# Attention scores of the last image in the scans' PSUM while a scan waits, and gates multiplied into the scans' sums

## The chip, the cores and the metric

The kernel runs on one core of one Trainium2 chip. The metric is the device time of one execution in microseconds (us); a kernel's time is the median of several runs. TensorE is written PE, VectorE DVE, ScalarE ACT, GpSimd POOL, and SyncE SP; SP issues nearly all DMAs here. PSUM has eight banks of 512 f32 per partition; SBUF has 128 partitions.

## What is computed

A batch of 4 images, each 32 x 32 x 256 in f32, that is 1024 rows of 256 channels, goes through four layers. Images meet nowhere.

```python
x = L0(x)   # norm, 256->512, depthwise 3x3, gelu; scan with 64 states per channel; norm, 512->256, add
x = L1(x)   # 1x1 256->128, grouped 3x3, 1x1 128->256, add, relu
t = t + attention(ln(t), edges)          # 8 heads of 32; the mask allows the given edges only
t = t + moe8(ln(t))                      # 8 experts of hidden 256, two chosen, all computed
# L3, attention slot: a scan with 16 states per channel
x_main, x_gate = split(ln(t) @ W_in)     # 512 channels each
u  = silu(x_main @ W_conv)
dt = softplus(u @ W_dt);  B, C = split(u @ W_bc)
h[t] = exp(dt[t] * A) * h[t-1] + dt[t] * B[t] * u[t]      # per channel and state
y[t] = sum over states of h[t] * C[t]
t = t + (y * silu(x_gate)) @ W_out
t = t + moe8(ln(t))                      # 8 experts of hidden 512
```

## The kernel before

**Two programs in one.** `Hybrid.run` writes one instruction stream from two Python generators. `scans` emits the eight recurrences one after the other, in the order of `SCANS`: (0,0), (0,1), (3,0), (0,2), (3,1), (0,3), (3,2), (3,3), a pair being layer and image. `STAGES` is the side work: `front` (L0 up to its scan), `middle` (the end of L0, L1, attention, the first experts, and L3 up to its scan, which is `front3`), and `last` (`back3`, then the second experts `moe(3, b, tb)` and the store of the image). At each `yield` of `scans`, `run` advances the side work by up to two ticks, as long as the estimated clocks of all engines (class `Metered`) stay behind that of DVE. So the order on every engine is fixed when the program is written.

**A scan's unit.** A unit is 128 partitions of (channel, state): 2 channels in layer 0, 8 channels in layer 3. There are 256 units in a scan of layer 0 and 64 in a scan of layer 3. For unit k the generator emits:

- `load(k)`, line 416: `dA`, the channels' dt rows, each spread over its states by a DMA of its own from SP: 2 DMAs in layer 0, 8 in layer 3. Tile `dA` has 5 buffers, so the DMAs of unit k wait until the scan of unit k-5 has been done.
- `decay(k)`: ACT takes exp of `dA` in place.
- `first(k)`: PE spreads dt*u from tile `S` into `ps_rep`, a tile of two PSUM banks (tag "x", 2 buffers: four banks).
- DVE multiplies `ps_rep` by the rows of B in place, and then makes the scan `h<-dA,ps_rep`; POOL multiplies `h` by the rows of C.
- `pair(k)`, for every second unit: PE sums over the states into `ps_y`. After the 8 units of a block of 64 channels (layer 3; 64 units in layer 0), ACT copies `ps_y` to `yo`, and SP stores it in DRAM (`y<-yo`, line 470, two DMAs).

In step k the order is `load(k + 4)`, `first(k + 1)`, `decay(k + 2)`, DVE's product for k, a yield, the scan and POOL's product for k, and, where k is odd, `pair(k - 2)`. So POOL has the product of unit k ahead of whatever `pair(k - 2)` gives it, and SP has `load(k + 4)` ahead of the stores of `pair(k - 2)` and `load(k + 5)` behind them.

**A scan that waits.** `chunk` loads tile `S` for a block of units, from `parts` that `front3` or `front` has written. Where these do not exist yet, and 5 units (`LATEST`) are left before them, `need` runs the side work to that point with no unit of a scan in between. This happens to (3,3): it waits for `middle` of image 3. The wait stands at the start of step 59 of scan (3,2).

**Attention of one pair of heads** (`heads`): for each of 8 blocks of keys, `scores` makes two score tiles `ps_sc` (tag "s", one bank each, 2 buffers) by three matmuls for each head (keys x queries in f32; the row maxima, in bf16; the mask, in bf16), and ACT takes exp of each into `p`. Then `values` adds four f32 matmuls with 32 columns of weights each (values and ones, for two heads) into `ps_at`. `pipe` emits `values` of a block before `scores` of the next one:

```python
for s in reversed(range(len(steps))):
    if 0 <= tick - s < len(items):
        steps[s](items[tick - s])
```

Four pairs of heads times two halves of the queries are eight calls for an image, 64 blocks of keys in all.

**The gate.** `front3` stores silu(x_gate) in DRAM as `gate`. `back3` loads it again for each of the four groups of 128 channels (`gate_back`, 512 KB each, line 1699), loads the sums (`y_back`, line 768), and POOL multiplies the one into the other in two halves (`gated`) before PE's projection `ps_o`.

Of the kernel before, what the change touches and what calls it, by code (L numbers as in the profile page):

```python
# [7 lines left out]
F32 = mybir.dt.float32  # L8
BF16 = mybir.dt.bfloat16
I32 = mybir.dt.int32  # L10
AF = mybir.ActivationFunctionType
ALU = mybir.AluOpType
# [4 lines left out]
P = 128  # L17
NB = 4
L = 1024
TB = L // P  # L20
C = 256
DI = 512
DC = DI // P
# [18 lines left out]
AHEAD = 12  # L42
LATEST = 5
# [89 lines left out]
class Hybrid:  # L133
# [217 lines left out]
    def scans(self, mp, psum):  # L351
# [14 lines left out]
            ]  # L366
        chunks, rows, waiting = {}, {}, []
        state = {}
        y = None

        def chunk(k):

# [21 lines left out]
                )  # L394
            chunks[scan, d] = S

        def chunks_ahead(k):

            if k + AHEAD < len(units) and units[k + AHEAD][2:] == (0, 0, 0):
                waiting.append(k + AHEAD)  # L400
            while waiting:
                scan, d = units[waiting[0]][:2]
                if waiting[0] - k > LATEST and ("parts", *scan, d) not in self.ready:
                    break
                chunk(waiting.pop(0))

        def load(k):
            if k >= len(units):
# [23 lines left out]
        def first(k):  # L432
            if k >= len(units):
                return
            scan, d, c, i, j = units[k]
            spread = self.tables[scan[0]][1]
            G = P // self.states[scan[0]]
            ps = psum.tile([P, L], F32, tag="x", name="ps_rep", bufs=2)
            for g in range(2):
                cols = slice(g * 512, (g + 1) * 512)  # L440
                nc.tensor.matmul(
                    ps[:, cols], lhsT=spread[:, i, :], rhs=chunks[scan, d][:, 2 * c + j, cols],
                    start=True, stop=True,
                )
            state[k] = (state[k], ps)

        def pair(k):

            nonlocal y
            scan, d, c, i, j = units[k]  # L450
            n = self.states[scan[0]]
            per = 32 * n // P
            collect = self.tables[scan[0]][2]
            if i == 0:
                y = psum.tile([P, 512], F32, tag="y", name="ps_y", bufs=1)
            h = [state.pop(k - 1), state.pop(k)]
            for g in range(2):
                for j in range(2):
                    at = 32 * (2 * g + j)
                    nc.tensor.matmul(  # L460
                        y[at : at + 32, :], lhsT=collect[:, i, :],
                        rhs=h[j][:, g * 512 : (g + 1) * 512],
                        start=(i == 0), stop=(i == per - 1), tile_position=(0, at),
                    )
            if i == per - 1:
                yo = mp.tile([P, 512], F32, tag="yo", name="yo", bufs=2)
                nc.scalar.copy(yo, y)
                to = self.keep(("y", *scan, d, c), [64, L])
                for g in range(2):
                    nc.sync.dma_start(to[:, g * 512 : (g + 1) * 512], yo[64 * g : 64 * g + 64, :])  # L470
                if c == 1:
                    self.done.add((scan, d))
# [6 lines left out]
        decay(1)  # L479
        first(0)  # L480
        for k in range(len(units) + 4):
            chunks_ahead(k)
            load(k + 4)
            first(k + 1)
            decay(k + 2)
            if k < len(units):
                a, inp = state.pop(k)
                B, Cm = rows[units[k][0]]
                nc.vector.tensor_tensor(inp, inp, B, ALU.mult)
            yield  # L490
            if k < len(units):
                h = mp.tile([P, L], F32, tag="h", name="h", bufs=5)
                nc.vector.tensor_tensor_scan(h, a, inp, 0.0, ALU.mult, ALU.add)
                nc.gpsimd.tensor_tensor(h, h, Cm, ALU.mult)
                state[k] = h
            if k % 2 == 1 and 2 <= k < len(units) + 2:
                pair(k - 2)
            yield

    def need(self, scan, d):  # L500
# [34 lines left out]
    def run(self):  # L535

        self.done, self.ready = set(), set()
        self.todo, self.stage, self.wait = list(STAGES), None, None
        nc, tc = self.nc, self.tc
        with tc.tile_pool(name="scan", bufs=1) as mp, tc.tile_pool(  # L540
            name="scps", bufs=1, space=PSUM
        ) as psum, tc.tile_pool(name="sdps", bufs=1, space=PSUM) as side, tc.manual_schedule():
            self.side_psum(side)
            self.mask_work, self.sorted = self.mask_prepare(), False
            clock = self.clock = dict.fromkeys(Metered.COST, 0.0)
            self.nc = Metered(nc, clock)
            for n, _ in enumerate(self.scans(mp, psum)):
                if n % 2:
                    next(self.mask_work, None)
                now = clock["vector"]  # L550
                for e in clock:
                    clock[e] = max(clock[e], now - LAG)
                for _ in range(TICKS):
                    if max(clock.values()) > clock["vector"] + LEAD or self.advance() is None:
                        break
            while self.advance() is not None:
                pass
            self.nc = nc
        assert not self.todo
# [742 lines left out]
    def heads(self, fp, raw, sums, qT, kT, v, maskT, mT, nh, hp):  # L1302

        nc = self.nc
        qs = slice(nh * 512, (nh + 1) * 512)
        c, at = hp // 2, 64 * (hp % 2)
        acc = self.psum.tile([P, 512], F32, tag="acc", name="ps_at", bufs=1)
        got = {}  # L1310

        def scores(kb):
            two = [self.psum.tile([P, 512], F32, tag="s", name="ps_sc", bufs=2) for _ in range(2)]
            rows = [slice(at + 32 * i, at + 32 * i + 32) for i in range(2)]
            for i in range(2):
                nc.tensor.matmul(
                    two[i], lhsT=kT[rows[i], c, kb * P : (kb + 1) * P], rhs=qT[rows[i], c, qs],
                    start=True, stop=False,
                )
            for i in range(2):  # L1320
                nc.tensor.matmul(
                    two[i], lhsT=self.onesb[rows[i], :], rhs=mT[rows[i], c, qs],
                    start=False, stop=False,
                )
            for i in range(2):
                nc.tensor.matmul(
                    two[i], lhsT=self.identb, rhs=maskT[:, kb, qs], start=False, stop=True
                )
            got[kb] = p = fp.tile([P, 2, 512], F32, tag="p", name="p", bufs=3)
            for i in range(2):  # L1330
                nc.scalar.activation(p[:, i, :], two[i], AF.Exp)

        def values(kb):
            p = got.pop(kb)
            for i in range(4):
                h = 2 * hp + i % 2
                nc.tensor.matmul(
                    acc[32 * i : 32 * i + 32, :],
                    lhsT=v[:, kb, h * HD : (h + 1) * HD] if i < 2 else self.ones,
                    rhs=p[:, i % 2, :],  # L1340
                    start=(kb == 0), stop=(kb == TB - 1), tile_position=(0, 32 * i),
                )

        yield from self.pipe(range(TB), scores, values, cost=1.3, cut=True)
        nc.scalar.copy(raw[at : at + 64, c, :], acc[:64, :])
        nc.scalar.copy(sums[at : at + 64, c, :], acc[64:, :])

# [343 lines left out]
    def back3(self, b, tb):  # L1691
        nc, tc = self.nc, self.tc
        with tc.tile_pool(name=f"h{b}", bufs=1, side="right") as sp:
            nc.sync.dma_start(tb, self.mem["t", b])
            y = sp.tile([P, DC, L], F32, name="y_back")
            gate = sp.tile([P, DC, L], F32, name="gate_back")

            def fetch(d):
                nc.sync.dma_start(gate[:, d, :], self.mem["gate", b, d])
                yield from self.scanned((3, b), y, d)  # L1700

            def gated(d):
                for g in range(2):
                    cols = slice(g * 512, (g + 1) * 512)
                    nc.gpsimd.tensor_tensor(y[:, d, cols], y[:, d, cols], gate[:, d, cols], ALU.mult)
                    yield 0.8

            yield 1.0
            yield from fetch(0)
            w_out = self.weight(sp, "L3_attn_W_out", DC)  # L1710
            yield from self.add_rows(tb, self.bout3, TB)
            for d in range(1, DC):
                yield from fetch(d)
                for _ in range(4):
                    yield 0.5
                yield from gated(d - 1)
            for _ in range(4):
                yield 0.5
            yield from gated(DC - 1)
            got = {}  # L1720

            def project(j):
# [95 lines left out]
```

## Time and profile before

| | |
|---|---|
| median of 3 runs | 6822.12 us (6815.66 to 6823.56) |
| profiled execution | 6818.64 us, of which the span of its instructions is 6816.9 us |
| busy, share of the span | PE 79%, DVE 77%, POOL 54%, ACT 51% |
| TensorE clock granted, mean | 0.828 |
| exp of scores, `p<-ps_sc` 128x512 | 512 times, 594 ns |
| POOL, `y_back<-y_back,gate_back` 128x512 | 32 times, 1266 ns (median) |
| POOL, `h<-h,rows` 128x1024 | 1280 times, 2372 ns |
| DMA issues of `dA` | 2048 of 256 KB and 2048 of 64 KB |
| attention of image 3, `ps_sc` | from 5505.4 to 5764.0 us |

Nearly every instruction has line 124, a wrapper through which all engines are called. So groups are told apart by their tiles' names, and only DMA issues by their lines. In a row of the timeline the first two numbers are the start and the length in us, and "[2.80 <-PE ps_sc L124]" means that the engine had been idle for 2.80 us and that PE's work on `ps_sc` ended this. An f32 matmul is recorded as two instructions, a bf16 matmul as one.

### The profile page before, as it was taken

The page shows a single profiled execution, that of the slowest core. Times are in us where ns is not written, and L with a number is a line of the kernel's source. Part 1 is how long each engine was busy: PE and PEld are TensorE (multiplying, and loading weights), DVE is VectorE, ACT ScalarE, POOL GpSimd, SP SyncE. Part 2 cuts the span into 40 slices and gives each one's busy share as a digit, 9 for nine tenths or more (in the row PEclk, how much of TensorE's full clock was granted, in tenths as well). Part 3 has the DMA queues.
Part 4 walks back from the last instruction along what each step waited for, and adds up shares of the span by engine and source line. Part 5 has one row for each costly group of instructions (what it writes and reads, how often), then busy time and mean ns, then how long its engine had stood idle before and what let it go on. Part 6 is the DMA issues. An engine that isn't in the chain of part 4 may idle for free. (4 is left out here: it accounts for less than half of the span.)

```text
span 6816.9 us, 65916 instructions
## 1 busy us (share of the span) xinstructions
PE 5387.2 (79%) x20320; PEld 2164.2 (32%) x20320; DVE 5225.0 (77%) x4486; ACT 3449.8 (51%) x4152; POOL 3651.6 (54%) x1801
## 2 busy tenths in 40 slices
PE   6558778579797568979689679798698687967979
PEld 3003213122242022234145222243253222523556
DVE  8778988988798987889889977798899861247411
ACT  2426666445476334557568345477485443245411
POOL 0876786755457655555856555557666540054200
PEclk8558779689798578979789689798698789877989
DMA  2556665754365665446756655366666640146321
GB/s 72 147 144 161 178 173 154 194 138 119 102 169 162 182 156 143 115 120 177 192 144 163 178 150 129 103 161 169 171 170 178 155 117 7 45 134 148 84 62 34
DMA packets 394235, 937.44 MB, mean 138 GB/s; under 512 B 83220, under 2 KB 165728, under 8 KB 392224
## 3 DMA queue, kind: packets, MB, share of 16 engines
q1 hardware_dynamic: 391696, 930.53, 51.3%
q8 instruction: 172, 2.82, 0.2%
q0 software_dynamic: 2128, 2.13, 0.2%
q14 instruction: 239, 1.96, 0.1%
HBM read 842.59 MB, written 93.95 MB: 137 GB/s over the span
## 5 line engine op out<-in xcount | busy, mean ns | idle before, releaser
L124 POOL TENSOR_TENSOR h<-h,rows 128x1024 f32<-128x1024 f32 x1280 | 3032.7, 2372 | 1995.8 <-DVE h L124 1649.5
L124 DVE TENSOR_TENSOR_SCAN h<-dA,ps_rep 128x1024 f32<-128x1024 f32 x1280 | 2925.3, 2285 | 238.9 <-issue 105.6
L124 DVE TENSOR_TENSOR ps_rep<-ps_rep,rows 128x1024 f32<-128x1024 f32 x1280 | 1552.9, 1213 | 289.0 <-PE ps_rep L124 288.8
L124 ACT ACTIVATE dA<-dA,A_L_conv_A_log 128x1024 f32<-128x1024 f32 x1024 | 1153.5, 1145 | 727.9 <-DMA dA<-dt 673.5
L124 PE MATMUL ps_rep<-S,spread_L_conv_A_log 96*128 96x512 bf16 x2048 | 765.6, 465 | 743.6 <-DVE h L124 710.4
L124 PE MATMUL ps_y<-h,collect_L_conv_A_log 128*32 128x512 f32 x4096 | 802.2, 761 | 95.5 <-POOL h L124 93.5
L124 PE MATMUL ps_h<-xTm,we 128*128 128x512 f32 x1536 | 719.0, 607 | 3.8 <-ACT h_m L124 2.2
L124 PE MATMUL ps_e<-we,h_m 128*128 128x256 f32 x3072 | 702.3, 381 | 8.1 <-ACT h_m L124 6.4
L124 ACT ACT_TABLE_LOAD x495 | 635.1, 1283 | 74.8 <-PE ps_h L124 44.3
L124 PEld LDWEIGHTS <-spread_L_conv_A_log 96*128 96x128 bf16 x2048 | 161.5, 103 | 1523.6 <-DVE h L124 1220.7
L124 PEld LDWEIGHTS ps_e<-we,h_m 128*128 128x128 f32 x3072 | 581.3, 190 | 155.4 <-issue 45.7
L124 ACT ACTIVATE p<-ps_sc 128x512 f32<-128x512 f32 x512 | 277.8, 594 | 549.9 <-PE ps_sc L124 537.4
L124 DVE SCALAR_TENSOR_TENSOR tb<-ps_e,cw,tb 128x256 f32<-128x256 f32 x512 | 220.6, 474 | 404.3 <-PE ps_e L124 404.3
L124 ACT ACTIVATE h_m<-ps_h,cols 128x512 f32<-128x512 f32 x384 | 260.7, 687 | 473.6 <-PE ps_h L124 470.9
L124 ACT ACTIVATE dA<-dA,A_L_attn_A_log 128x1024 f32<-128x1024 f32 x256 | 293.3, 1148 | 384.8 <-DMA dA<-dt 342.8
L124 PE MATMUL ps_at<-p,v 128*32 128x512 f32 x1024 | 374.6, 610 | 64.6 <-ACT p L124 53.8
L124 PEld LDWEIGHTS ps_h<-xTm,we 128*128 128x128 f32 x1536 | 291.7, 193 | 341.4 <-issue 294.2
L124 PE MATMUL ps_rep<-S,spread_L_attn_A_log 96*128 96x512 bf16 x512 | 184.4, 449 | 195.2 <-DVE h L124 177.1
L124 PE MATMUL ps_sc<-qT,kT 32*128 32x512 f32 x1024 | 295.2, 649 | 44.8 <-ACTq L1234 26.0
L124 PE MATMUL ps_at<-p,ones 128*32 128x512 f32 x1024 | 272.1, 610 | 0.0
L124 PEld LDWEIGHTS ps_y<-h,collect_L_conv_A_log 128*32 128x32 f32 x4096 | 107.4, 119 | 492.4 <-POOL h L124 243.3
L124 PE MATMUL ps_cv<-pad,diag 128*128 128x512 f32 x576 | 260.4, 593 | 0.0
(306 smaller groups left out, 4945.8 us busy)
## 6 DMA issues: line engine op xcount, KB each, us to landing
dA<-dt SPq DMA_DIRECT2D x2048, 256.0 KB
dA<-dt SPq DMA_DIRECT2D x2048, 64.0 KB
we<-in_L_ffn_W_dram SPq DMA_DIRECT2D x64, 512.0 KB
parts<-parts SPq DMA_DIRECT2D x64, 384.0 KB
S<-parts SPq DMA_DIRECT2D x96, 256.0 KB
dt<-sp_r SPq DMA_DIRECT2D x64, 256.0 KB
y<-yo SPq DMA_DIRECT2D x128, 128.0 KB
y_back<-y SPq DMA_DIRECT2D x64, 256.0 KB
```

The source lines that it names most:

```text
L124: return got(*args, **kw)
```

## The change

1. **Scores in the scans' PSUM.** `chunks_ahead` no longer stops at the start of step k. Where the `parts` are missing it says so, the step goes on without `first(k + 1)`, and at the end of the step the wait is made, with `self.alone` set, and then `first(k + 1)`. A call of `heads` that begins meanwhile puts the scores of both heads into one tile of tag "x" (`ps_sx`, two banks, two buffers), takes exp of both in one activation of 128x1024, and emits through a pipe with an empty step, so that `values` of a block comes behind `scores` of the next one.
2. **Gates beside the scan.** In `pair`, a scan of layer 3 loads a tile `gate` (128x512, one buffer; two DMAs of 128 KB) at the first pair of each block of 64 channels, and POOL multiplies it into `yo` behind ACT's copy; the stores follow. `back3` neither loads nor multiplies gates any more; `W_out` is loaded first there, and the ticks of the multiplications are gone.

The order of the instructions shows which work is affected: 40 of the kernel's 256 blocks of keys go over (80 of 512 score tiles, 40 activations `p<-ps_sx`), that is the last five of image 3's eight calls; 32 POOL products `y_back` become 32 products `yo`; 16 loads `gate_back` become 64 loads `gate_y`. The number of matmuls stays the same. The last unit of (3,2) whose input `ps_rep` is emitted before the wait is number 59 in both programs (units counted from 0), and the side work has 8027 matmuls ahead of that point before and 8007 after, 10 of them to a block of keys.

```diff
@@ scans
+        self.scan_psum = psum
+        y = gate = None
...
-        def chunks_ahead(k):
-            if k + AHEAD < len(units) and units[k + AHEAD][2:] == (0, 0, 0):
+        def chunks_ahead(k, late=False):
+            if not late and k + AHEAD < len(units) and units[k + AHEAD][2:] == (0, 0, 0):
                 waiting.append(k + AHEAD)
             while waiting:
                 scan, d = units[waiting[0]][:2]
-                if waiting[0] - k > LATEST and ("parts", *scan, d) not in self.ready:
-                    break
+                if ("parts", *scan, d) not in self.ready:
+                    if waiting[0] - k > LATEST:
+                        break
+                    if not late:
+                        return True
+                    self.alone = True
                 chunk(waiting.pop(0))
+                self.alone = False
+            return False
...
             if i == 0:
                 y = psum.tile([P, 512], F32, tag="y", name="ps_y", bufs=1)
+                if scan[0] == 3:
+                    gate = mp.tile([P, 512], F32, tag="gate", name="gate_y", bufs=1)
+                    for g in range(2):
+                        nc.sync.dma_start(
+                            gate[64 * g : 64 * g + 64, :],
+                            self.mem["gate", scan[1], d][64 * c : 64 * c + 64, g * 512 : (g + 1) * 512],
+                        )
...
                 nc.scalar.copy(yo, y)
+                if scan[0] == 3:
+                    nc.gpsimd.tensor_tensor(yo, yo, gate, ALU.mult)
...
-            chunks_ahead(k)
+            waits = chunks_ahead(k)
             load(k + 4)
-            first(k + 1)
+            if not waits:
+                first(k + 1)
...
                 pair(k - 2)
+            if waits:
+                chunks_ahead(k, True)
+                first(k + 1)
             yield
@@ heads
+        alone = self.alone
...
-            two = [self.psum.tile([P, 512], F32, tag="s", name="ps_sc", bufs=2) for _ in range(2)]
+            if alone:
+                both = self.scan_psum.tile([P, 2, 512], F32, tag="x", name="ps_sx", bufs=2)
+                two = [both[:, i, :] for i in range(2)]
+            else:
+                two = [self.psum.tile([P, 512], F32, tag="s", name="ps_sc", bufs=2) for _ in range(2)]
...
+            if alone:
+                nc.scalar.activation(p, both, AF.Exp)
+                return
             for i in range(2):
                 nc.scalar.activation(p[:, i, :], two[i], AF.Exp)
...
-        yield from self.pipe(range(TB), scores, values, cost=1.3, cut=True)
+        if alone:
+            yield from self.pipe(range(TB), scores, lambda kb: None, values, cost=1.3)
+        else:
+            yield from self.pipe(range(TB), scores, values, cost=1.3, cut=True)
@@ back3
             y = sp.tile([P, DC, L], F32, name="y_back")
-            gate = sp.tile([P, DC, L], F32, name="gate_back")
-
-            def fetch(d):
-                nc.sync.dma_start(gate[:, d, :], self.mem["gate", b, d])
-                yield from self.scanned((3, b), y, d)
-
-            def gated(d):
-                for g in range(2):
-                    cols = slice(g * 512, (g + 1) * 512)
-                    nc.gpsimd.tensor_tensor(y[:, d, cols], y[:, d, cols], gate[:, d, cols], ALU.mult)
-                    yield 0.8
-
-            yield 1.0
-            yield from fetch(0)
             w_out = self.weight(sp, "L3_attn_W_out", DC)
+            yield 1.0
+            yield from self.scanned((3, b), y, 0)
             yield from self.add_rows(tb, self.bout3, TB)
             for d in range(1, DC):
-                yield from fetch(d)
-                for _ in range(4):
-                    yield 0.5
-                yield from gated(d - 1)
+                yield from self.scanned((3, b), y, d)
             for _ in range(4):
                 yield 0.5
-            yield from gated(DC - 1)
```

More of the change, by code (lines that the diff above doesn't have):

```diff
@@ L368, in scans @@
         state = {}
-        y = None
+        self.scan_psum = psum
+        y = gate = None
         def chunk(k):
@@ L447, in pair @@
         def pair(k):
-            nonlocal y
+            nonlocal y, gate
             scan, d, c, i, j = units[k]
@@ L538, in run @@
         self.todo, self.stage, self.wait = list(STAGES), None, None
+        self.alone = False
         nc, tc = self.nc, self.tc
@@ L1324, in scores @@
                 )
+            got[kb] = p = fp.tile([P, 2, 512], F32, tag="p", name="p", bufs=3)
             for i in range(2):
@@ L1328, in scores @@
                 )
-            got[kb] = p = fp.tile([P, 2, 512], F32, tag="p", name="p", bufs=3)
+            if alone:
+                nc.scalar.activation(p, both, AF.Exp)
+                return
             for i in range(2):
@@ L1695, in back3 @@
             y = sp.tile([P, DC, L], F32, name="y_back")
-            gate = sp.tile([P, DC, L], F32, name="gate_back")
-            def fetch(d):
-                nc.sync.dma_start(gate[:, d, :], self.mem["gate", b, d])
-                yield from self.scanned((3, b), y, d)
-            def gated(d):
-                for g in range(2):
-                    cols = slice(g * 512, (g + 1) * 512)
-                    nc.gpsimd.tensor_tensor(y[:, d, cols], y[:, d, cols], gate[:, d, cols], ALU.mult)
-                    yield 0.8
+            w_out = self.weight(sp, "L3_attn_W_out", DC)
             yield 1.0
-            yield from fetch(0)
-            w_out = self.weight(sp, "L3_attn_W_out", DC)
+            yield from self.scanned((3, b), y, 0)
             yield from self.add_rows(tb, self.bout3, TB)
             for d in range(1, DC):
-                yield from fetch(d)
-                for _ in range(4):
-                    yield 0.5
-                yield from gated(d - 1)
+                yield from self.scanned((3, b), y, d)
             for _ in range(4):
                 yield 0.5
-            yield from gated(DC - 1)
             got = {}
```

## The prediction

> **What bounds the kernel now.** I read the 40 slices first, then the chain that ended last, then the timeline and the waits of the stretches that the change touches. In the slices, DVE is busy for some 80% up to slice 32; then the scans have nothing to do:
>
> ```profile
> PE   6558778579797568979689679798698687967979
> ...
> DVE  8778988988798987889889977798899861247411
> ```
>
> DVE's scans follow each other with gaps of at most 18 us, save one: unit 58 of (3,2) starts at 5592.1, unit 59 at 6048.8. In between, image 3 runs alone; its last five calls of `heads` fill the time from 5607.1 (ACT's copy `raw`) to 5766.5, the copy of the last call: 159.3 us. The table of busy time by stretch (us, then PE, PEld, DVE, ACT, POOL, clock, DMA share, GB/s):
>
> ```profile
> 5600.00:5767.00 167.00, 144.58 (x688) 36.45 (x684) 11.07 (x18) 55.57 (x102) 7.55 (x6) 1.00 0.01 2
> 6071.00:6385.00 314.00, 231.61 (x844) 105.45 (x845) 245.40 (x202) 157.60 (x163) 171.89 (x82) 0.76 0.61 157
> ```
>
> PE looks full in the first row, but the timeline of one block of keys shows a loop through ACT:
>
> ```profile
> 5626.46 1.13 PE L124 MATMUL ps_sc<-qT,kT 32*128 32x512 f32 x4
> 5627.42 0.38 PE L124 MATMUL ps_sc<-mT,onesb 32*128 32x512 bf16 x2
> 5627.74 0.60 PE L124 MATMUL ps_sc<-maskT,identb 128*128 128x512 bf16 x2
> 5628.22 1.09 ACT L124 ACTIVATE p<-ps_sc 128x512 f32<-128x512 f32 x2 [2.80 <-PE ps_sc L124]
> 5628.87 1.10 PE L124 MATMUL ps_at<-p,v 128*32 128x512 f32 x3 [0.53 <-ACT p L124]
> ...
> 5630.35 1.13 PE L124 MATMUL ps_sc<-qT,kT 32*128 32x512 f32 x4
> ```
>
> Scores, exp, values, scores: 3.89 us a block, all on the path, since nothing else can go on.
>
> Afterwards the chain is PE's experts to the end, with one hole where image 3's last stage begins:
>
> ```profile
> 6510.21 4.44 DMA out_dram<-tb
> ...
> 6517.48 10.01 DMA gate_back<-gate
> 6527.50 10.22 DMA y_back<-y
> 6537.88 1.27 POOL y_back L124
> ```
>
> In the scans of layer 3, SP is nearly full: eight issues a unit. In (3,1), 3873 to 4179 us, it waited for a free `dA` only this long (us, times, longest), and elsewhere issues stand end to end:
>
> ```profile
> SPq L416 <- DVE h L124: 17.5, 17, 3.6
> ```
> ```profile
> 4111.15 1.09 SPq L470 DMA_DIRECT2D y<-yo  x2
> 4112.34 8.44 SPq L416 DMA_DIRECT2D dA<-dt  x16
> ```
>
> **The change part by part**, against the profiled execution (6818.64 us; its span is 6816.9, the median of the runs 3.5 above it).
>
> *Scores.* With values a block later, PE has in order: scores k, values k-1, scores k+1, values k. Scores issue from 5626.46 to the second mask matmul's end of issue, 1.71 us (three matmuls of two heads; the next weights could go at 5628.17). Values that had `p` in time, earlier in the same attention, took 0.97, from 5523.40 to 5524.37:
>
> ```profile
> 5523.40 0.60 PE L124 MATMUL ps_at<-p,v 128*32 128x512 f32 x2
> 5523.41 0.60 PE L124 MATMUL ps_at<-p,ones 128*32 128x512 f32 x2
> ```
>
> So PE's floor is 2.69 us a block. The one exp of 128x1024 has no row from PSUM; the two halves took 1.09 together, `dA` of the same width 1.15. I take 1.15, at no cost: it lies beside values and scores of 2.69 us. Where that cover is gone, at the end of each call, PE waits about 0.45. Five calls: 40 x 2.69 + 5 x 0.45, plus 3.7 for `ps_wo` between them, are 113.6 instead of 159.3: **-45.7**. Bounds: nothing gained, if ACT still ends each block; -50.
>
> The row that bears on the clock is the first of the table: granted 1.00 throughout, although PE pauses 0.53 us in each block. A rule speaks against this part. The Trainium skill's page "TensorE: Matmul & The Clock Gate", section "A second HAM failure mode: psum-queue depth-cycling", says that going round PSUM banks can leave PE such short pauses that its clock swings between half and full; at half clock the 40 blocks would take 215 us, and the sum would turn to a loss. I go by the row.
>
> *Side work two blocks behind.* Ahead of the same unit 59 there are 8007 matmuls of side work instead of 8027, two blocks of keys. They now run in the wait, two by 3.89, less what the scans save without them (3.6 instead of 4.3 us for two units): **+6.4**, bounds 0 and 7.8.
>
> *Unit 59 before the wait.* One unit less after it, 6048.80 to 6052.23: **-3.4**; at worst 0.
>
> *Gate, into the scans.* Per block of 8 units SP gets two issues more (1.1, as the stores' 1.09) and its stores wait longer: for POOL's product (1.27 and 0.15 of signalling) behind ACT's copy, or behind POOL's `h` of unit k where that is later. Behind the waiting stores are `load(k + 5)` and all later ones; ACT's `decay` and then the scan wait for these. From the trace's times of the copies and of `h`, the stores of the four scans are released 11.5, 11.5, 11.8 and 8.1 us later in sum; with 8.8 for the issues each scan has about 20 us more on SP. Not all of it is lost: SP pays back where it waited for a buffer, and `dA` lies ready 2 to 5 us before its scan in quiet units, 7 to 18 behind side work on DVE. Carried from unit to unit by these two numbers, the lag delays the scans by 7, 7, 4 and 8 us: **+26**. Bounds 0 and 78. The gate's own DMAs wait for the product of the block before (one buffer), which the stores ahead of them have waited for already. On POOL, the product holds up `h` of unit k+1: by 1.3 us, and where ACT's copy comes late (it ended up to 5.2 us after `h` of unit k) by up to 2.8. I cost this at nothing, since POOL was busy for 170 us of 306 in (3,1), PE takes that `h` only three steps later, and `h` has five buffers; without that room PE, which reads `ps_y`'s inputs in order, would lose 1 to 3 us a block, which I leave within the upper bound.
>
> *Gate, out of `back3` of image 2.* Between 6109 and 6165 the scan (3,3) waits for `dA` behind `tb`, `W_out`, `y_back` and `gate_back`:
>
> ```profile
> 6152.53 2.29 DVE L124 TENSOR_TENSOR_SCAN h<-dA,ps_rep 128x1024 f32<-128x1024 f32 x1 [5.16 <-DMA dA<-dt]
> ```
>
> DVE's gaps there sum to 25 us. Gates are 2 of 5.5 MB; but the three last `y_back` pairs now come in one clump. I take a third, **-8**, bounds 0 and -25. The stage's ticks fall from 33 to 13, yet the order puts only 8 more matmuls before the scan's last unit; 24 are 13.8 us in the experts' stretch behind it: at most -4.6, I take **-3**. In images 0 and 1 the ticks come out even again within the scan, and DVE had its `dA` there: 0, within 5 either way.
>
> *Image 3's `back3`.* 5.5 MB landed from 6514.7 to 6537.7, 0.24 MB/us; 3.5 MB take 14.6 us, and the product of 1.27 goes too. PE starts `ps_o` at about 6529.5 instead of 6539.2: **-9.7**, bounds -1.4 and -12. Late next is PE itself.
>
> Sum: -45.7 + 6.4 - 3.4 + 26 - 8 - 3 - 9.7 = -37.4; 6781 for a profiled execution, 6785 for the median.
>
> **Rivals.** (a) *SP bounds the scans of layer 3.* If what SP gets more is lost whole, 78 instead of 26, the sum is +14.6: 6837, slower. For it: 17.5 us of waiting in 306, less than the 20 that come. Against: `dA` was mostly ready ahead of its scan, and DVE's stalls for side work give SP time. It decides from 16 us a scan on. (b) *Scores gain half*: the exp ends PE's waits after all, or weight loads keep a block at 3.3 us; then -23 there and -15 in all, 6807, at the edge of what a measurement tells. For it: PE's floor is put together from two places; against: both were recorded in the same attention at full clock. (c) *The gate is free*: 5-deep `dA` swallows everything, and the clump costs nothing: -63 to -75, about 6753. (d) That the change doesn't do what it says is excluded: the order has the forty activations of 1024.
>
> **How the numbers follow.** Forecast 0.66, (a) 0.11, (b) 0.11, (c) 0.12. The forecast's own range, with 38 to 50 for the scores and 12 to 40 for the gate, is 6767 to 6807. The range reaches up towards (a) and down over (c): 6750 to 6820 leaves out (a) and a few of the rest. About 0.2%, 13.6 us, is what a measurement tells from no change. Faster: forecast, (c) and a share of (b), 0.80; same: the rest of (b) and the low part of (a), 0.10; slower 0.10.
>
> **What would show it.** After: a block in the wait from one `ps_sx` score to the next in 2.7 us, ACT's exp about 1.1 long without PE idle before `ps_at`; the wait's gap in DVE some 40 us shorter than 456.7; scans (3,0) and (3,1) at 318 and 313 us up to the start of the next scan, instead of 310.6 and 305.9; SP's waits for `DVE h` there gone, and waits of line 470 for POOL; PE's `ps_o` of image 3 about 20 us after the store of image 2. Wrong: half clock in the wait, blocks above 3.3 us, or scans of layer 3 longer by 16 us or more.

## The result, and the profile after

The changed kernel takes 6839.83 us (median of 9 runs, 6828.76 to 6856.88), the kernel before 6822.12 beside it: a ratio of 1.0031, 95% interval 1.0019 to 1.0043. It is slower by 0.3%. The profiled execution has a span of 6834.1 us against 6816.9, that is 17.2 more, at a granted clock of 0.826 against 0.828.

The slices look as before; the scans' long hole on DVE is in the 34th and 35th:

```profile
PE   6558778679797567979789668798698678867989
...
DVE  8778988988798986789899977788899871247511
```

Stretch by stretch, from the starts of DVE's scans (the first two columns give the time from a scan's first unit to the next scan's first):

| stretch | before | after | difference |
|---|---|---|---|
| start to the first scan | 207.4 | 204.9 | -2.5 |
| (3,0) | 310.6 | 326.2 | +15.6 |
| (3,1) | 305.9 | 326.7 | +20.8 |
| (0,0), (0,1), (0,2), (0,3) together | 4491.9 | 4491.5 | -0.4 |
| (3,2), with the wait | 755.5 | 738.2 | -17.3 |
| (3,3), first to last unit | 306.1 | 323.3 | +17.2 |
| last unit of (3,3) to the end | 439.4 | 423.2 | -16.2 |

The wait does what it was to do. DVE's gap in it is 425.0 us instead of 456.7. The last five calls of image 3 take 125.8 us instead of 159.3 (ACT's copies `raw`, 5662.4 to 5788.2), and the timeline of PE has a block of keys from one score to the next in 2.81 us, with `values` of the block before behind the scores:

```profile
5715.98 1.13 PE L124 MATMUL ps_sx<-qT,kT 32*128 32x512 f32 x4
5716.95 0.38 PE L124 MATMUL ps_sx<-mT,onesb 32*128 32x512 bf16 x2
5717.26 0.60 PE L124 MATMUL ps_sx<-maskT,identb 128*128 128x512 bf16 x2
5717.80 0.62 PE L124 MATMUL ps_at<-p,v 128*32 128x512 f32 x2
...
5718.79 1.13 PE L124 MATMUL ps_sx<-qT,kT 32*128 32x512 f32 x4
```

Within a call PE no longer stops for `p`. The end does what it was to do as well. In the chain of the work that ended last there is no `gate_back` between the store of image 2 and `ps_o`, and from the one to the other it is 20.7 us instead of 29.0:

```profile
6534.98 4.47 DMA out_dram<-tb
6540.03 6.48 DMA w_L_attn_W_out<-in_L_attn_W_out_dram
6546.52 9.03 DMA y_back<-y
6555.69 14.34 PE ps_o L124 x58
```

All this is given away by the four scans of layer 3. What SP waited for in (3,1), at the stores before (3873 to 4179 us; total, times, longest):

```profile
SPq L470 <- ACT yo L124: 6.3, 4, 2.0
```

and at the stores and the loads after, 3885 to 4212 us:

```profile
SPq L489 <- POOL yo L124: 14.9, 5, 5.3
SPq L425 <- DVE h L124: 14.3, 8, 3.6
```

Line 489 is the stores of `yo`, 425 the loads of `dA`. The stores now wait for POOL's product, 15.3 us with all their waits instead of 6.5, and the 16 issues of `gate_y` take 9.5 us, counted from each start to the next: 18 us more on SP, and the scan is 20.8 longer. SP's wait for a free `dA` (`DVE h`) fell only from 17.5 to 14.3: some 3 us were paid back there. Where the engines lose the rest, by the waits of ACT and DVE in (3,1), before:

```profile
ACT dA L124 <- DMA dA<-dt: 73.0, 24, 8.3
...
DVE ps_rep L124 <- PE ps_rep L124: 30.4, 23, 6.7
DVE h L124 <- DMA dA<-dt: 13.2, 28, 7.8
...
DVE lnt_w L124 <- ACT lnt_r L124: 2.1, 1, 2.1
```

and after:

```profile
ACT dA L124 <- DMA dA<-dt: 95.3, 27, 7.7
...
DVE ps_rep L124 <- PE ps_rep L124: 38.4, 23, 12.2
DVE h L124 <- DMA dA<-dt: 13.3, 23, 4.9
DVE lnt_w L124 <- ACT lnt_r L124: 6.6, 1, 6.6
```

DVE itself waits no longer for `dA`. ACT does, 22.3 us longer, in the decays that stand two units ahead of the scan. DVE then waits for others: 8.0 us longer for PE's `ps_rep`, and 11 us longer ahead of its own side work (19.3 instead of 8.0 us over all such rows, of which the largest, `lnt_w`, is shown), where ACT or PE is late.

### The profile page after: what moved, and what is told of

It is laid out like the page before. It is cut to its first block, busy times and chain, and to the rows that moved or that the text cites. A ratio compares the mean times of both kernels' runs of the same rounds, so it can differ in the third digit from the quotient of the medians.

```text
span 6834.1 us, 65860 instructions
## 1 busy us (share of the span) xinstructions
PE 5346.9 (78%) x20236; PEld 2150.1 (31%) x20320; DVE 5219.0 (76%) x4486; ACT 3442.2 (50%) x4108; POOL 3649.1 (53%) x1801
## 5 line engine op out<-in xcount | busy, mean ns | idle before, releaser
L124 ACT ACTIVATE p<-ps_sc 128x512 f32<-128x512 f32 x432 | 234.4, 594 | 460.6 <-PE ps_sc L124 313.8
L124 PE MATMUL ps_at<-p,v 128*32 128x512 f32 x1024 | 352.7, 623 | 67.0 <-ACT p L124 59.3
L124 PE MATMUL ps_sc<-qT,kT 32*128 32x512 f32 x864 | 252.0, 657 | 50.4 <-ACTq L1258 43.6
```

Source lines behind the costliest of these rows:

```text
L124: return got(*args, **kw)
```

## The experiments

**Theory.** In the scans of layer 3 SP's new issues and its stores' wait are lost whole; scores and `back3` gain as meant. **Rivals**: the order of the side work has moved; POOL's product holds up the sums and the scans, whatever SP does; SP does pay back and something else costs.

Differences below are between the medians of a kernel and of the kernel before that was run beside it (6818 to 6821 us); in brackets stands the 95% interval of the ratio. The changed kernel's difference is +17.7. Lengths of scans are in us, measured as in the table above, from one profiled execution of each kernel. (0,3), which no edit of the kernel before, the changed one and the four parts touches, took 1134.2 to 1137.2 in these six, so differences of 3 us between scans say little.

### The change in parts

*Scores alone*: the diff's `chunks_ahead`, `heads` and the order in `scans`, with `back3` and `pair` as before.

> The kernel before with the scores' part of the change alone (back3 keeps its gates). Theory: the score part does what it was to do, only less, and costs the scans nothing: DVE's gap in the wait 32 to 40 us shorter than 456.7, the scans of layer 3 as long as before (310.6, 305.9), the median 28 to 38 us lower. Rival (the moved order of the side work, not the gates, makes the scans of layer 3 longer): (3,0) and (3,1) 10 us longer or more here too, and the median within 15 us of the kernel before.

6781.91 us, -37.5; ratio 0.9950 (0.9936 to 0.9963). Scans (3,0) and (3,1) take 310.2 and 309.3 us, DVE's gap in the wait 411.9 (behind unit 59 here, behind 58 before). The five calls take 121.2 us. The gap is 44.8 shorter, somewhat more than the theory said, and in (3,0) and (3,1) the order of the side work is not the cause. In (3,3) it may have a part: that scan takes 312.3 us instead of 306.1 without any gate in it.

*Gate alone*: `pair` and `back3` of the change, the rest as before.

> The kernel before with the gate part alone. Theory (SP is the bound in the scans of layer 3, so its new issues and waits are lost whole): each scan of layer 3 15 to 21 us longer, 65 to 70 in all, 16 less at the end; the median 42 to 55 us higher. Rival (as forecast, SP pays back): scans longer by 26 in all, median 5 us higher or less.

6876.80 us, +57.4; ratio 1.0085 (1.0072 to 1.0098). The scans are 19.2, 25.5, 20.4 and 13.0 us longer, 78 in sum, more than the 65 to 70 of the theory; the end is 20.5 shorter. Scores and gate alone sum to +19.9, the change to +17.7: the two parts hardly meet.

*Loads alone*, and *product alone*, each in the kernel before:

```diff
@@ loads alone: pair
+                if scan[0] == 3:
+                    gate = mp.tile([P, 512], F32, tag="gate", name="gate_y", bufs=1)
+                    for g in range(2):
+                        nc.sync.dma_start(gate[64 * g : 64 * g + 64, :], ...)
@@ product alone: scans, pair
+        one = mp.tile([P, 512], F32, name="one_y")
+        nc.gpsimd.memset(one, 1.0)
...
                 nc.scalar.copy(yo, y)
+                if scan[0] == 3:
+                    nc.gpsimd.tensor_tensor(yo, yo, one, ALU.mult)
```

> The kernel before with the loads of gate_y in pair alone: 64 DMAs more, nothing reads them, back3 keeps its gates. Theory: SP's issues are the bound, 16 x 0.58 = 9.3 us for each scan of layer 3, 30 to 40 us in all, at the median too. Rival 1 (POOL's product and the waits for it make all of the loss): 0 to 8 us. Rival 2 (SP pays back half from its waits for a free buffer): 15 to 22 us.

> The kernel before, with POOL multiplying yo by a tile of ones in the scans of both layers ahead of the stores; no gate is loaded, back3 keeps its gates. Theory: the stores wait 8 to 15 us longer in each scan of layer 3, in front of the loads of dA, and this is lost too: 25 to 40 us in all; together with the loads alone about the loss of the gate part's scans, 65 to 70. Rival (only issues count, the wait falls where SP would have waited for a free buffer): 0 to 8 us.

(The second text says "both layers"; the edit has the product in layer 3 alone.) Loads: 6858.95 us, +39.6; ratio 1.0063 (1.0050 to 1.0076); the first three scans longer by 5.2, 10.1 and 10.1 us, (3,3) by 10.1. Product: 6865.02, +45.7; ratio 1.0078 (1.0065 to 1.0091); scans longer by 12.5, 13.8, 8.5 and -0.9, and SP's wait at the stores in (3,1) is 17.5 us instead of 6.5. Behind the last unit of (3,3) the product's kernel loses another 12.0 us, to which no run here gives a cause. So 16 issues a scan, 9.5 us of SP, cost about that much (35.5 in the four scans), and one product of 1.27 us per block about as much (33.9). Both rivals that named a single culprit fail.

### Taking the load off SP again

*Stores later* (in the changed kernel): `pair` puts its stores on a list, and they are issued two units later.

```diff
-                for g in range(2):
-                    nc.sync.dma_start(to[:, g * 512 : (g + 1) * 512], yo[64 * g : 64 * g + 64, :])
+                def out(to=to, yo=yo, scan=scan, d=d, c=c):
+                    ...
+                late.append((k + 4 if scan[0] == 3 else k + 2, out))
@@ scans, behind pair(k - 2)
+            while late and late[0][0] <= k:
+                late.pop(0)[1]()
```

> The changed kernel with the stores of yo in layer 3 put two units later on SP, behind two more loads of dA, when POOL's product has been done. Theory (the stores' wait holds the loads behind it): SP's wait at the stores falls from 15 to 18 us a scan to under 4, scans of layer 3 10 to 15 us shorter than in the changed kernel, median 6780 to 6800. Rival (SP then waits as long for a free dA): the wait moves to the loads of dA, and the median stays within 10 us of the changed kernel.

6792.73 us, -26.1; ratio 0.9958 (0.9943 to 0.9974); scans 318.8 and 315.4. The stores' wait in (3,1) is gone; about half of it, 8 us, came back as waiting for a free `dA` (`DVE h`, 22.5 instead of 14.3), so this rival was right in part.

*One DMA for two*, without and with the late stores:

```diff
-                    for g in range(2):
-                        nc.sync.dma_start(gate[64 * g : 64 * g + 64, :], ...)
+                    nc.sync.dma_start(
+                        gate,
+                        self.mem["gate", scan[1], d][64 * c : 64 * c + 64, :].rearrange("p (g t) -> g p t", g=2),
+                    )
...
+                nc.sync.dma_start(to.rearrange("p (g t) -> g p t", g=2), yo)
```

> The changed kernel with one DMA instead of two for each load of gate_y and each store of yo: SP has the 16 issues for a scan of layer 3 that it had before the change, the same bytes move. Theory (the issues on SP are lost whole): each scan of layer 3 8 to 10 us shorter than in the changed kernel (326.2, 326.7), the median 30 to 40 us below it, 6800 to 6810. Rival (it is the bytes of the gates, or their wait for the buffer, not the issues): within 8 us of the changed kernel, 6832 to 6848.

> Both together: stores two units later, and one DMA for each load of gate_y and each store. Theory (issues and wait add up on SP): scans of layer 3 about as long as before the change (306 to 312 us), the median about 6765 to 6785, where the scores' part alone gave 6782 and the gates give 16 back at the end. Rival (POOL's product holds up the sums, and these the scan, whatever SP does): scans stay 8 us or more above those before, median above 6795.

7132.10 us (ratio 1.0451, 1.0435 to 1.0468) and 7070.68 (1.0362, 1.0347 to 1.0378): the kernels are slower, where both theories had them faster. In the first kernel scan (3,1) takes 395.6 us. The largest waits of SP in it, 3989 to 4385 us, are loads of `dA` that wait for such DMAs; in the changed kernel there are no such rows:

```profile
SPq L425 <- DMA gate_y<-gate: 44.7, 8, 7.9
SPq L425 <- DMA y<-yo: 28.1, 7, 4.0
```

*Two issues for eight channels of `dA`*, in layer 0 one for two:

```diff
-            for g in range(G):
+            m = min(G, 4)
+            for g in range(0, G, m):
...
-                    self.mem["dt", *scan, d][r : r + 1, :].to_broadcast([n, L]),
+                    self.mem["dt", *scan, d][r : r + m, :].unsqueeze(1).to_broadcast([m, n, L]),
```

> The changed kernel with two DMAs for the eight channels of a unit's dA in layer 3 instead of eight (four channels of 16 states each, the same bytes): some 390 issues of SP less in each scan of layer 3. Theory (SP bounds these scans, in the kernel before too): they fall well below those before the change, to 235 to 290 us, where DVE's two instructions a unit (3.5 us) or PE and ACT end the units; median 6500 to 6720. Rival (SP was not the bound, DVE waits for dA because of DMA bandwidth or the engines' order): scans 310 us or more, median above 6790.

13616.71 us, twice the time. Busy time by stretch (PE, PEld, DVE, ACT, POOL, clock, DMA share, GB/s), in scan (0,0) of this kernel:

```profile
300.00:1200.00 900.00, 241.09 (x662) 56.01 (x658) 301.57 (x199) 143.28 (x163) 269.56 (x154) 0.55 0.16 60
```

and of the changed one:

```profile
300.00:1200.00 900.00, 670.48 (x2003) 184.98 (x2000) 795.15 (x535) 503.00 (x642) 657.39 (x345) 0.75 0.60 160
```

The DMA engines are busy for 0.16 of their time, as if little more than two of the sixteen worked. The Trainium skill has a reason, page "DMA: Bandwidth & Descriptors", section "Rules for kernel authors": a DMA is spread by its slowest dimension, and one with an outermost dimension below 16 stays on at most so many engines. Here it was 2 in layer 0 (4 in layer 3, and 2 for the gates and sums of the two kernels ahead), where the loads before have 16 or more. 2 of 16 is 0.125, and the row with 0.16 fits; no run tells the single engines apart. So these three runs measure the spread of a DMA and not SP's issues, and say nothing on the theory.

*Plain layouts*: the gates and sums of layer 3 lie in DRAM as the tiles do, 128 rows of 512; `front3` stores a gate in four DMAs and `back3` loads `y_back` in four for two. Without, and with, the late stores:

```diff
+                    nc.sync.dma_start(gate, self.mem["gate", scan[1], d][c])
...
+                if scan[0] == 3:
+                    nc.sync.dma_start(to, yo)
```

> The changed kernel with gates and sums of layer 3 laid out in DRAM as the tiles of a block stand (128 rows of 512), so that one plain DMA loads gate_y and one stores yo: again the 16 issues for a scan that SP had before the change, but each DMA keeps one piece of 128 rows; front3 stores a gate in four DMAs and back3 loads y_back in four instead of two, outside these scans for the most part. Theory (issues on SP are lost whole): scans (3,0) and (3,1) 8 to 10 us shorter than in the changed kernel (326), the median 25 to 37 us below it, 6803 to 6815. Rival (bytes or buffer waits of the gates, not issues): within 8 us of it.

> The same with the stores of yo two units later as well. Theory (issues and the stores' wait add up on SP): scans (3,0) and (3,1) as before the change, 304 to 312 us; the median 6755 to 6775. Rival (POOL's product holds up the sums and so the scans): scans 316 us or more, median 6785 or more.

Plain: 6796.59 us, -24.1; ratio 0.9965 (0.9954 to 0.9977); scans 321.9 and 319.1, that is 4.3 and 7.6 shorter than in the changed kernel, less than the 8 to 10 of the theory, though the median fell by more than it said. Plain and late: 6763.79, -56.9; ratio 0.9922 (0.9908 to 0.9935); scans 309.3 and 308.3, before the change 310.6 and 305.9. In profiled time plain takes 37.4 us off the changed kernel, late stores 36.9, both together 75.2. With the issues and the wait off SP, the gate's bytes and POOL's product cost the scans nothing. The rival with POOL falls.

*ACT as a second issuer*: of `gate_y` (with the late stores), and of two of the eight `dA` loads:

```diff
@@ first
-                        nc.sync.dma_start(
+                        nc.scalar.dma_start(
                             gate[64 * g : 64 * g + 64, :],
@@ second: load
-                nc.sync.dma_start(
+                (nc.sync if g % 8 < 6 else nc.scalar).dma_start(
                     a[g * n : (g + 1) * n, :],
```

> The changed kernel with the stores two units later, and the gate_y loads issued by ACT instead of SP. Theory: SP is the bound and ACT is not, so the 16 issues for a scan cost nothing there: scans (3,0) and (3,1) at 305 to 312 us, the median 6755 to 6775. Rival (ACT, which must turn dA into decays, pays for the issues as SP did): 6785 to 6800, as with late stores alone.

> The changed kernel with two of the eight dA loads of each unit of layer 3 issued by ACT: 128 of SP's 512 issues for a scan, 66 us at 0.52, the same DMAs otherwise. Theory (SP's issue time is the bound of these scans): they become 30 us shorter or more (under 296), until DVE or ACT ends the units; the median under 6740. Rival (bandwidth or latency of dA, not issues): scans within 8 us of 326, the median 6820 or more.

6864.07 us (+43.4; ratio 1.0065, 1.0047 to 1.0082) and 6864.95 (+44.3; 1.0066, 1.0051 to 1.0080). The scans take 340.1 and 339.9 us in the first kernel, 334.7 and 330.9 in the second. Both theories fail; the second rival comes close by its numbers, but its reason need not be the right one, since SP now waits for DMAs that ACT issues late. The largest of SP's waits in (3,1), first kernel:

```profile
SPq L425 <- DMA gate_y<-gate: 32.3, 9, 11.7
```

and second:

```profile
SPq L425 <- DMA dA<-dt: 47.9, 47, 10.2
```

In the trace these DMAs take eight semaphores in turn, and each waits for the one before it on its semaphore. Where that one is ACT's, SP stands until ACT has issued it and it has landed: in the first kernel's longest wait SP stands from 4211.91 for 11.7 us, and ACT issues at 4220.91; in the second's from 4060.97 for 10.2 us, and ACT issues at 4066.30. ACT's own time for its issues, 1.14 us for a pair of `gate_y`, may cost the scans too; no run separates the two. The same page's section "Issuing engines are not separate DMA queues" says that several issuers save only the time of issuing; here not even that was saved. These two are inconclusive on whether SP's issues bound the scans.

### Why so little was paid back

> The changed kernel with six buffers of dA instead of five, load(k + 5) in step k, LATEST 6, and one buffer of yo instead of two to make room. Theory (the forecast's pay-back failed because five buffers let SP run ahead too little: it waits 17 to 21 us of a scan for a free dA while ACT waits for dA elsewhere): SP's waits for a free buffer and ACT's waits for dA fall by 10 us a scan or more, scans (3,0) and (3,1) 310 to 320 us instead of 326, median 6795 to 6825. Rival (SP's issue time alone sets the scans): ACT's waits only move, scans within 5 us of 326, median 6830 or more.

> The changed kernel with decay(k + 1) instead of decay(k + 2) in step k. Theory (a late dA is lost through ACT: it stands in the decay two units ahead of the scan, and the side work's activations and PE behind them are late): ACT's waits for dA in (3,1), 95.3 us, fall by 30 or more, scans (3,0) and (3,1) 8 to 20 us shorter than 326, median 6795 to 6825. Rival (a late dA is lost at the scan itself): the decay then ends just ahead of the scan, scans as long or longer, median 6835 or more.

```diff
@@ six buffers
-LATEST = 5
+LATEST = 6
-            a = mp.tile([P, L], F32, tag="dA", name="dA", bufs=5)
+            a = mp.tile([P, L], F32, tag="dA", name="dA", bufs=6)
-            load(k + 4)
+            load(k + 5)
-                yo = mp.tile([P, 512], F32, tag="yo", name="yo", bufs=2)
+                yo = mp.tile([P, 512], F32, tag="yo", name="yo", bufs=1)
@@ decay a unit later
             load(k + 4)
+            decay(k + 1)
             ...
-            decay(k + 2)
```

Six buffers: 6787.27 us, -30.7; ratio 0.9953 (0.9939 to 0.9966); scans 314.0 and 319.5 instead of 326.2 and 326.7, with the same issues on SP. Decay later: 6822.39, +4.4; ratio 1.0003 (0.9994 to 1.0013); scans 315.2 and 315.7, while (0,2) and (0,3) became 10 and 5 us longer. ACT's wait for `dA` in (3,1) was 95.3 us in the changed kernel. With six buffers it is

```profile
ACT dA L124 <- DMA dA<-dt: 66.3, 17, 10.8
```

and with the decay later, where DVE's own wait grows (13.3 in the changed kernel),

```profile
ACT dA L124 <- DMA dA<-dt: 56.0, 13, 9.9
...
DVE ps_rep L124 <- PE ps_rep L124: 26.3, 16, 7.4
DVE h L124 <- DMA dA<-dt: 21.8, 27, 7.6
```

So much of the lag is lost through ACT: moving its decays alone gives 11 us of each of these scans back, DVE's wait for `ps_rep` falls from 38.4 to 26.3, and its waits ahead of its own side work from 19.3 to 9.9. How much is less sure, since this profiled execution was the fastest of eleven, 13 us under their median; by the medians the kernel is 13 us faster than the changed one. And a deeper prefetch does pay back. With six buffers SP waited for `DVE h` 5.0 us in (3,1) instead of 14.3, and the stores for POOL 8.7 instead of 14.9; with as many issues on SP the scans are shorter, so SP's issue time alone is not what sets them.

### A version that beats both

> Plain layouts, stores two units later, and six buffers of dA. Theory: the scans of layer 3 fall below those before the change (310.6, 305.9) by 5 to 15 us, median 6715 to 6755. Rival (SP's issue time alone): scans as with plain and late, 308, median 6758 to 6772.

6745.89 us, -72.1; ratio 0.9887 (0.9872 to 0.9902). Scans 305.0 and 307.6. It has all of the change, plain layouts, late stores and six buffers of `dA`. The first scan gains as expected, the second does not.

## Why the prediction was wrong

**The step that failed is "Gate, into the scans"**, and in it the pay-back. The load on SP was rightly counted: about 20 us a scan, 78 in all. The prediction let SP pay most of it back where it waits for a free `dA`, and where `dA` lies ready 2 to 5 us ahead of its scan, and took 26. The gate alone cost 78 in the scans, the whole upper bound; in the changed kernel they are 69 longer: 15.6, 20.8 and 17.2, and 15.4 in (3,2), where unit 58 starts 291.7 us after the first instead of 276.2. Of SP's waits for `DVE h` in (3,1), which were to be gone, 14.3 of 17.5 us are still there. Of the 17.2 in (3,3), 6.2 were there with the scores alone. Two things were overlooked:

- The slack was measured at the scan. The first to need `dA` is ACT, two units earlier, and ACT has side work queued behind its decay. What is late there is late for PE's side work, which stands ahead of `ps_rep`, and for DVE's own. The chain is SP, ACT, then PE or DVE's side work, then the scan; on DVE it looks like a wait for PE or for ACT.
- SP's waits for a free buffer are no store of time. SP can use them only if it may run further ahead, and five buffers end that. With six, part came back. Nor were they all of SP's waits: the view that gives the 17.5 us in (3,1) has 46 in all, 20 of them for DMAs, so the issues do not stand end to end elsewhere, as the prediction read them.

Rival (a) had the price, 6837 against 6839.8 measured, and its trigger, 16 us a scan, was met or all but met in each of the four. That the two agree to 3 us is partly luck: the scans lost 69 instead of its 78, but the five calls gave 33.5 instead of 45.7, and the end 16.2 instead of 12.7. And its mechanism holds only for five buffers of `dA`: the load was lost nearly whole, but with six the same issues cost less.

**Scores**: the mechanism was right, the size 8 us off. Predicted 113.6 us for the five calls, measured 121.2 with the scores alone and 125.8 with all. The term was mis-sized in two places: a block is 2.81 instead of 2.69 (PE's floor was put together from two rows; 40 blocks make +4.8), and `ps_wo` with what follows costs 7.7 instead of 3.7. There ACT first makes the norm of the queries that are done, in the changed kernel from 5733.04 to 5737.87, and then the clock halves (with the scores alone for one block of 4.40 us instead of 2.81). The ends of the calls cost 1.2 less in all. ACT's norm, and PE, which waits behind it:

```profile
5733.04 1.28 ACT L252 ACT_TABLE_LOAD   x1
...
5735.80 2.07 ACT L124 ACTIVATE y_at<-y_at,lny_b,lny_r 128x256 f32<-128x256 f32 x4 [1.03 <-DVE lny_b L124]
...
5740.17 1.07 PE L124 MATMUL ps_at<-p,v 128*32 128x512 f32 x2 [2.41 <-ACT p L124]
...
5742.03 2.08 PE L124 MATMUL ps_sx<-qT,kT 32*128 32x512 f32 x4
```

**The clock** was taken as 1.00. Behind that pause it is not: the score matmuls take 2.08 us instead of 1.13. By stretch (columns as in the prediction's table):

```profile
5742.00:5746.00 4.00, 4.00 (x16) 0.99 (x16) 0.45 (x1) 0.46 (x1) 1.41 (x2) 0.50 0.00 0
5765.50:5788.20 22.70, 22.20 (x127) 5.35 (x130) 0.00 (x0) 9.35 (x10) 0.00 (x0) 1.00 0.00 1
```

The prediction weighed a rule of the Trainium skill, "TensorE: Matmul & The Clock Gate", section "A second HAM failure mode: psum-queue depth-cycling", on frequent short pauses of PE between groups of matmuls. It did not come about here: the blocks, without their pauses of 0.53, ran at 1.00. Half clock came once, with one pause of 2.41 us, and this call took 27.6 us instead of 22.7. With the scores alone the call after the same pause took 23.1.

**Unit 59 and the side work two blocks behind** (+6.4 and -3.4) cannot be told apart in the traces. Wait and scores together were -42.7 in the sum; the scores alone gave -37.5, and the 5 us between lie within the 8 by which the five calls were mis-sized.

**Gate, out of `back3`**: the end is 16.2 us shorter where -9.7 and -3 were predicted; from the store of image 2 to `ps_o` -8.3. The -8 for image 2's `back3` stands among the losses of (3,3) and can at most be seen with SP free: 306.9 us with plain and late against 312.3 with the scores alone. Against the 306.1 before the change nothing of it shows.

## What to carry to other kernels

Slack is to be read at the first consumer of a tile and not at the one that makes the result; whoever else is queued behind that consumer gets the delay. A queue that issues for most of a stretch is a resource like an engine: in these scans each issue and each wait put into it was lost nearly whole with five buffers, and a deeper prefetch won part of it back. So put a store that must wait behind loads that need not, lay out in DRAM what saves an issue, and do not save it with a DMA whose outermost dimension is as small as 2 or 4.

## What the runs showed of the hardware

- A DMA with an outermost dimension of 2 holds up those behind it on the queue: 16 of them in a scan of layer 3 (each 256 KB, in place of 32 of 128 KB) made the scan 69 us longer, 326.7 to 395.6, that is 4.3 us each. SP waited 72.8 us for them.
- An issue of 64 KB on SP is 0.42 us long (median in (3,1)) and takes 0.46 from start to start; 488 of them make 226 of 306 us.
- The clock fell to 0.50 with a PE pause of 2.41 us in the wait, and stayed there for a time that differs between kernels with the same order there: 3.4 us (scores alone), 6.8 (plain and late), 10.2 (the last version) and 13.7 (the changed kernel); the call behind the pause took 23.1, 24.7, 26.3 and 27.6 us, instead of 22.7. Not every such pause does it: in the kernel before, PE paused for 2.67 us up to 6028.93, and the clock was 1.00 from 6020 to 6032.
